# One block of the scan's input formed by TensorE with B on diagonals, and the scan's PSUM tiles by halves

## The chip, the cores and the metric

The kernel runs on one core of one Trainium2 chip. The metric is the time of one execution on the device in microseconds (us). Everything is in fp32.

## What is computed

Two layers follow each other on 8 images of 64 x 64 x 192. The first (a state-space block with a local convolution and an MLP) is not touched. The second is a two-dimensional selective scan. For each of four directions k it runs over L = 4096 positions, for 384 channels with 16 states each:

```python
def step(hst, inp):
    d, bm, cm, uu = inp
    dA = jnp.exp(d[..., None] * A[None])
    dBu = (d * uu)[..., None] * bm[:, :, None, :]
    hst = dA * hst + dBu
    y = jnp.einsum('bkdn,bkn->bkd', hst, cm)
    return (hst, y)
```

`d` is the step size of a channel, `uu` its input, `bm` and `cm` are the B and C of the position, one number for each state. The change is about how `dBu` is formed: the product of `d * uu` (a channel and a position) with B (a state and a position).

## The kernel before

The second layer goes through the images one after the other. A front (projection, 3 x 3 convolution, stores to DRAM in three layouts) comes first, mixed with the finish of the image before. Then `main()` in `scan` runs alone: it is an order written out by hand, kept on every engine.

The scan of an image has 32 **steps**: four directions k, eight chunks of 512 positions (`TT`). A step has 24 **units**: 8 pairs of states p, times 3 groups d of 128 channels. A unit works on two tiles of 128 partitions (the halves f = 0, 1): 2 states x 64 channels on the partitions, 512 positions along the row. Units of a step are numbered 0 to 23 in this document, and iteration u is what the loop in `main` issues for unit u. In iteration u these instructions go out:

- SP: `load_c` (every third unit) loads C of the next pair, broadcast over 64 partitions, into `cb` (three buffers).
- DVE: `run(u)` makes two scans, `hs` from the decay `ea` and the input `g`, each over 512 positions (L1633).
- POOL: `run(u)` copies the last column to `cy` (L1645) and multiplies `hs` with `cb` to `hc` (L1647).
- ACT: `decay(u + 2)` makes `ea` by two exponentials of `dr`, the step sizes repeated over the partitions (L1606). Then come 3, 3 or 2 calls of `weigh` (L1591). One call takes a block j of 128 positions of `duT` (d * uu with positions on the partitions, 384 channels along the row) and scales it with one column of `bt`, which is B of one state with positions on the partitions. It writes one half of `pw`. A pair of states needs 4 blocks x 2 states = 8 calls, and the `todo` list runs ahead of their use by 10 calls.
- PE: `supply(u + 1)` turns the eight blocks of `pw` (2 halves x 4 blocks, 128 x 128 each) by transposes into the PSUM tile `g` of the next unit (L1617). `collect(u - 1)` then sums `hc` over the two states by a product with `sel`, into `y` (L1662); both halves of `y` are 64 columns wide. In direction 0 the first pair adds the skip term first (L1660).
- The pieces of `prepare(s + 1)`, which make the next step's inputs, are hung on fixed units: `project` (PE, `p_d`) on 2, 3 and 4, `keep` (DVE copy to `xdbl`, store of C to DRAM) on 5, `turn_b` on 6, `keep_b` and `step(0)` (PE, `p_dt`) on 7, and so on to 17; copies to `dr` on 11, 20 and 21.

The PSUM tiles of `g` are `[128, 2, 512]`, two banks, and there are two of them. All PSUM is used: four banks for `g`, three for `y`, one for the pieces.

All DMAs of the scan are issued from SP, in the order of the program; an issue that waits holds up what is behind it.

Of the kernel before, what the change touches and what calls it, by code (L numbers as in the profile page):

```python
# [8 lines left out]
F32 = mybir.dt.float32  # L9
AF = mybir.ActivationFunctionType  # L10
ALU = mybir.AluOpType
PSUM = bass.MemoryType.PSUM
DRAM = bass.MemoryType.DRAM
# [4 lines left out]
TT = 512  # L18
# [6 lines left out]
DT = DIN // 128  # L25

K, N, R = 4, 16, 12
NS1 = NT
NB1 = TT // 128
NP1 = N // 2  # L30

EXPLN = "natural_log_exp_and_others"

# [60 lines left out]
class Flow:  # L94
# [24 lines left out]
    def pool(self, tag, n):  # L119
        self.slots[tag] = [0.0] * n  # L120
# [911 lines left out]
def layer1(tc, consts, x1s, mv1, out, w_in, w_x, w_dt, w_out):  # L1032
    nc = tc.nc
# [6 lines left out]
    with ExitStack() as ctx:  # L1040
# [3 lines left out]
        mp = pool("m1", 1, space=PSUM)  # L1044
        dp = pool("d1", 3, space=DRAM)
        ddp = pool("dd1", 2, space=DRAM)
        yacc = pool("ya1", 1, side="right").tile([128, DT, L], F32, name="yacc")

        wi = wp.tile([CP, CT, 2 * DIN], F32, name="wi1")
# [28 lines left out]
        for m in range(2 * DT):  # L1078
            for ct in range(CT):
# [4 lines left out]
                    start=ct == 0,  # L1084
# [3 lines left out]
        nc.vector.tensor_copy(gb.rearrange("p m b -> p (m b)"), pb[:, : 2 * DT * nb])  # L1088
        keeper = []
        o = lambda ins: keeper[-1](ins)  # L1090

        def scaled(w, b, half):

# [340 lines left out]
        def scan(xo):  # L1434
# [7 lines left out]
            def spool(name, bufs, **kw):  # L1442
                pools[name] = cx.enter_context(tc.tile_pool(name=name, bufs=bufs, reuse_waits="tile", **kw))

            steps = [(k, c) for k in range(K) for c in (range(NS1) if k < 2 else range(NS1 - 1, -1, -1))]
            units = [(s, p, d) for s in range(len(steps)) for p in range(NP1) for d in range(DT)]
            state = [dict() for _ in steps]
            made = {}

# [3 lines left out]
            def prepare(s, bank=lambda name: mp.tile([128, TT], F32, name=name, tag="mm")):  # L1453
# [31 lines left out]
                def keep():  # L1485
                    xd = xds[s % 2]
                    o(nc.vector.tensor_copy(xd[0:44], st["p_d"][:44]))
                    st["cd"] = dp.tile([N, TT], F32, name="cd")
                    o(nc.sync.dma_start(out=st["cd"], in_=xd[16:32]))

                def turn_b():
                    xd = xds[s % 2]
# [43 lines left out]
                def keep_du(d):  # L1536
# [10 lines left out]
                    2: [(project, 0)],  # L1547
                    3: [(project, 1)],
                    4: [(project, 2)],
                    5: [(keep,)],  # L1550
                    6: [(turn_b,)],
                    7: [(keep_b,), (step, 0)],
                    8: [(soft, 0)],
# [56 lines left out]

            def supply(u):
                s, p, d = units[u]
                made["g", u] = g = pools["g1"].tile([128, 2, TT], F32, name="g")
                for f in range(2):
                    for j in range(NB1):
                        o(
                            nc.tensor.transpose(  # L1617
                                g[:, f, j * 128 : j * 128 + 128],
                                state[s]["pw", p, j][:, 2 * d + f].rearrange("p a b -> p (a b)"),
                                ident,  # L1620
                            )
                        )

            def run(u):
                s, p, d = units[u]
                k, c = steps[s]
                st = state[s]
                ea, g = made.pop(("e", u)), made.pop(("g", u))
                h = pools["h1"].tile([128, 2, TT], F32, name="hs")
                rev = (lambda ap: ap) if k < 2 else (lambda ap: ap[:, ::-1])  # L1630
                for f in range(2):
                    o(
                        nc.vector.tensor_tensor_scan(  # L1633
                            rev(h[:, f]),
                            rev(ea[:, f]),
                            rev(g[:, f]),
                            0.0 if first(s) else state[s - 1]["cy"][:, p, d, f : f + 1],
                            ALU.mult,
                            ALU.add,
                        )  # L1640
                    )
                if "cy" not in st:
                    st["cy"] = pools["pr1"].tile([128, NP1, DT, 2], F32, name="cy")
                last = TT - 1 if k < 2 else 0
                o(nc.gpsimd.tensor_copy(st["cy"][:, p, d], h[:, :, last]))  # L1645
                made["hc", u] = hc = pools["h1"].tile([128, 2, TT], F32, name="hc")
                o(nc.gpsimd.tensor_mul(hc, h, bc(st["cb", p], 1, [128, 2, TT])))  # L1647

            def collect(u):
                s, p, d = units[u]  # L1650
                k, c = steps[s]
                st = state[s]
                if p == 0:
                    st["y", d] = pools["y1"].tile([128, TT], F32, name=f"y{d}")
                y = st["y", d]
                hc = made.pop(("hc", u))
                half = [slice(f * 64, f * 64 + 64) for f in range(2)]
                if p == 0 and k == 0:
                    for f in range(2):
                        o(nc.tensor.matmul(y[half[f]], dskip[:, d, half[f]], st["xc"][:, d], start=True, stop=False))  # L1660
                for f in range(2):
                    o(nc.tensor.matmul(y[half[f]], sel, hc[:, f], start=p == 0 and k > 0, stop=p == NP1 - 1))  # L1662

            def add(u):
                s, p, d = units[u]
                k, c = steps[s]
                if p == NP1 - 1:
                    ya = view(yacc, k, d, c * TT, TT)
                    yv = seq(state[s]["y", d], k)
                    if k == 0:  # L1670
                        o(nc.vector.tensor_copy(ya, yv))
                    else:
                        o(nc.vector.tensor_add(ya, ya, yv))


            todo = [
                (s, p, j, i) for s in range(len(steps)) for p in range(NP1) for j in range(NB1) for i in range(2)
            ]

            def prologue(f, mq, front_pools):  # L1680

                yield "wait", "front"
                front_pools.close()
                for name, n in (("pr1", 2), ("dr1", 4), ("pw1", 8), ("bc1", 3), ("e1", 3)):
                    spool(name, n)
                load_first = prepare(0, lambda name: mq.tile([128, TT], F32, name=name, tag="mm"))
                ready.update({fn.__name__: fn for at in sorted(load_first) for fn, *_ in load_first[at]})
                r = yield step("SP", 0.1, ready["load"])
                yield "take", "mm"
                r += 3.5  # L1690
                for d in range(DT):
                    r = yield step("PE", 0.95, lambda: ready["project"](d), r)
                r = yield step("DVE", 0.7, ready["keep"])
                f.give("mm", r)
                f.at["xd"] = r
                yield "take", "mm"
                yield step("PE", 0.6, ready["turn_b"])
                r = yield step("DVE", 0.2, ready["keep_b"])
                f.give("mm", r)
                f.at["bt"] = r  # L1700
                load_c(0, 0)
                for d in range(DT):
                    yield "wait", ("du", d)
                for t in todo[:10]:
                    yield step("ACT", 0.55, lambda: weigh(*t), f.free["ACT"])
                for u in range(2):
                    yield step("ACT", 1.35, lambda: decay(u), None, "explog")
# [17 lines left out]
                f.at["du", d] = r  # L1725

            def main():
                for name, n, kw in (("h1", 3, {}), ("y1", 1, dict(space=PSUM)), ("g1", 2, dict(space=PSUM))):
                    spool(name, n, **kw)
                supply(0)  # L1730
                rest = iter(todo[10:])
                nu = len(units)
                for u, (s, p, d) in enumerate(units):
                    if p == 0 and d == 0:
                        pieces = prepare(s + 1) if s + 1 < len(steps) else {}
                    s2, p2 = (s, p + 1) if p < NP1 - 1 else (s + 1, 0)
                    if s2 < len(steps) and d == 0:
                        load_c(s2, p2)
                    run(u)
                    if u + 2 < nu:  # L1740
                        decay(u + 2)
                    for _ in range((3, 3, 2)[d]):
                        if t := next(rest, None):
                            weigh(*t)
                    if u + 1 < nu:
                        supply(u + 1)
                    if u >= 1:
                        collect(u - 1)
                    if u >= 2:
                        add(u - 2)  # L1750
                    for f, *args in pieces.get(p * DT + d, ()):
                        f(*args)
                collect(nu - 1)
                add(nu - 2)
                add(nu - 1)
                cx.close()
# [136 lines left out]
```

## Time and profile before

| | us |
|---|---|
| median of 3 runs | 23702.0 |
| lowest, highest run | 23690.56, 23706.31 |
| the profiled execution's own time | 23706.31 |
| its span | 23706.3 |

The first layer takes up to about 4,780 us of the span. Each image's scan takes about 2,100 us (the first from 5009 to 7112 us), with a front of about 250 us between two of them. One step of the scan takes 66.5 us in direction 0 and 65.55 us in the three others.

How to read it: the page gives busy time, which is an average over all stages. For a change in the scan the rows of a stretch inside a scan are what counts. A row of the timeline is a start, a duration, an engine, a line, an operation and its tiles (out<-in), and in brackets the time that the engine had been idle before and what ended it. PE records carry a tail after the array has finished, so their ends overlap; starts of the weight loads (PEld) tell better when PE was free.

### The profile page before, as it was taken

How to read it: one execution, taken by the hardware profiler on the slowest of the kernel's cores; microseconds unless marked ns; L12 is line 12 of the kernel's file. 1: busy time of each engine (PE TensorE's matmuls, PEld its weight loads, DVE VectorE, ACT ScalarE, POOL GpSimd, SP SyncE). 2: the span in 40 equal slices, each digit the busy share in tenths (PEclk: the TensorE clock that was granted, in tenths of full speed). 3: DMA queues.
4: the chain of work that ended last, by engine and by line, in shares of the span. 5: the costliest groups of instructions: out<-in, count | busy, mean ns of one | idle time of the engine just before them, and what ended most of it. 6: DMA issues, size and time to landing. Idle time of an engine off the chain costs nothing.

```text
span 23706.3 us, 312102 instructions
## 1 busy us (share of the span) xinstructions
PE 21012.6 (89%) x100356; PEld 10233.4 (43%) x100356; DVE 21257.2 (90%) x22093; ACT 20961.7 (88%) x37466; POOL 16001.1 (67%) x12871
## 2 busy tenths in 40 slices
PE   8999999978888888888888888888888888888888
PEld 4444444434444444444444444444444444444444
DVE  7888888779998999899989998999899989998998
ACT  5666666679998999899989998999899989998998
POOL 1111111159995998599859986997699769976997
PEclk8999999989999999999999999999999999999999
DMA  1111111133233322332233233322333333333332
GB/s 51 44 44 44 45 45 46 36 101 81 82 78 112 81 81 77 110 82 81 77 108 81 81 80 111 81 81 78 108 81 82 84 102 81 82 86 100 82 82 67
DMA packets 1205983, 1859.70 MB, mean 78 GB/s; under 512 B 268960, under 2 KB 502336, under 8 KB 1195136
## 3 DMA queue, kind: packets, MB, share of 16 engines
q1 hardware_dynamic: 1204352, 1839.73, 28.5%
q8 instruction: 807, 13.22, 0.2%
q14 instruction: 824, 6.75, 0.1%
HBM read 1225.98 MB, written 210.50 MB: 61 GB/s over the span
## 4 chain that ended last, share of the span: by engine, by line
POOL 46%; PE 22%; ACT 13%; DVE 8%; issue 6%; DMA 3%; SPq 1%; POOLq 0%; ACTq 0%; DVEq 0%
POOL hc L1647 43%; ACT pw L1591 5%; ACT ea L1606 5%; POOL cy L1645 3%; PE p_f L955 3%; DVE xs L1201 2%; DMA xc<-xo 2%; PE p_x L448 2%; PE p_f L975 2%; PE y L1662 2%; PE p_o L872 1%; PE g L1617 1%; PE p_y L789 1%; PE p_d L1480 1%; PE p_z L531 1%
## 5 line engine op out<-in xcount | busy, mean ns | idle before, releaser
L1647 POOL TENSOR_TENSOR hc<-hs,cb 128x1024 f32<-128x1024 f32 x6144 | 14577.6, 2373 | 12.3 <-POOL cy L1645 10.5
L1633 DVE TENSOR_TENSOR_SCAN hs<-ea,cy,g 128x512 f32<-128x512 f32 x10752 | 13027.1, 1262 | 602.4 <-PE g L1617 408.7
L1591 ACT ACTIVATE pw<-duT,bt 128x384 f32<-128x384 f32 x16384 | 8875.4, 601 | 23.5 <-DVE duT L1538 23.5
L1606 ACT ACTIVATE ea<-dr,an 128x512 f32<-128x512 f32 x12288 | 8121.7, 709 | 186.9 <-DVE hs L1633 169.5
L1662 PE MATMUL y<-hc,sel 128*64 128x512 f32 x24576 | 6628.6, 618 | 1836.3 <-POOL hc L1647 1816.1
L1617 PEld LDWEIGHTS g<-ident,pw 128*128 128x128 f32 x49152 | 5288.2, 141 | 4335.1 <-issue 2666.3
L1617 PE MATMUL g<-ident,pw 128*128 128x128 f32 x49152 | 6788.1, 279 | 60.8 <-ACT pw L1591 29.3
L1645 POOL COPY cy<-hs 128x2 f32<-128x2 f32 x6144 | 1150.7, 187 | 3394.4 <-DMA out_x<-xl 1744.8
L1662 PEld LDWEIGHTS y<-hc,sel 128*64 128x64 f32 x24576 | 1226.6, 135 | 3250.6 <-POOL hc L1647 3025.0
L1633 DVE TENSOR_TENSOR_SCAN hs<-ea,g 128x512 f32<-128x512 f32 x1536 | 1764.2, 1203 | 160.9 <-PE g L1617 119.6
L365 POOL TENSOR_TENSOR s<-xs 96x512 f32<-96x512 f32 x64 | 121.7, 1902 | 2136.0 <-DVE xs L343 1846.6
L1201 DVE SCALAR_TENSOR_TENSOR xs<-pad,p,xs 128x4096 f32<-128x4096 f32 x192 | 860.9, 4484 | 48.0 <-ACT xs L1191 40.8
L1509 PE MATMUL p_dt<-xdbl,wd 13*128 13x512 f32 x1536 | 857.5, 639 | 41.8 <-DVE de L1522 39.9
L365 POOL TENSOR_TENSOR s<-sq 96x512 f32<-96x512 f32 x128 | 180.4, 1409 | 937.9 <-ACT sq L378 842.3
L1480 PE MATMUL p_d<-xc,wx 128*44 128x512 f32 x1536 | 788.7, 596 | 23.4 <-DMA xc<-xo 23.4
L343 DVE SCALAR_TENSOR_TENSOR x<-xx,p,x 96x512 f32<-96x512 f32 x1024 | 784.4, 815 | 15.2 <-ACT x L332 15.0
L955 PE MATMUL p_f<-h,wf 96*128 96x512 f32 x1536 | 757.2, 631 | 43.8 <-ACT zs L550 27.4
L343 DVE SCALAR_TENSOR_TENSOR xs<-xin,p,xs 96x512 f32<-96x512 f32 x1024 | 746.9, 768 | 3.6 <-ACT xs L332 3.6
L975 PE MATMUL p_f<-m,wf 128*96 128x512 f32 x1536 | 695.0, 603 | 0.0
L1531 PEld LDWEIGHTS p_du<-ident,de 128*128 128x128 f32 x3072 | 323.4, 141 | 610.1 <-DVE de L1522 406.3
L365 POOL TENSOR_TENSOR s<-x 96x512 f32<-96x512 f32 x64 | 109.1, 1704 | 690.3 <-DVE x L343 606.7
L448 PE MATMUL p_x<-h,wi 96*128 96x512 f32 x1024 | 559.4, 679 | 12.0 <-ACT h L405 12.0
(202 smaller groups left out, 19293.3 us busy)
## 6 DMA issues: line engine op xcount, KB each, us to landing
cb<-cd SPq DMA_DIRECT2D x4096, 128.0 KB
dr<-de SPq DMA_DIRECT2D x3072, 128.0 KB
xc<-xo SPq DMA_DIRECT2D x256, 768.0 KB
e<-csd SPq DMA_DIRECT2D x256, 384.0 KB
xl<-x SPq DMA_DIRECT2D x256, 384.0 KB
ut<-xo SPq DMA_DIRECT2D x128, 768.0 KB
ut<-xo SPq DMA_DIRECT2D x256, 384.0 KB
xo<-xs SPq DMA_DIRECT2D x48, 1024.0 KB
```

The lines of the kernel that those rows point to most:

```text
L343: nc.vector.scalar_tensor_tensor(im(out[:, ct]), tap(ct, j), w[:, ct, j : j + 1], im(out[:, ct]), ALU.mult, ALU.add)
L448: nc.tensor.matmul(ps, wi[:, ct, 390 + mt * 128 : 518 + mt * 128], h[:, ct], start=ct == 0, stop=ct == 1)
L955: nc.tensor.matmul(ps, wf1[:, ct, mt * 128 : mt * 128 + 128], h[:, ct], start=ct == 0, stop=ct == 1)
L975: nc.tensor.matmul(ps[:CP], wf2[:, kt, ct * CP : ct * CP + CP], m[:, kt], start=kt == 0, stop=kt == 5)
L1201: nc.vector.scalar_tensor_tensor(xs, tap(j), kw[:, d, j : j + 1], xs, ALU.mult, ALU.add)
L1591: nc.scalar.activation(st["pw", p, j][:, :, i], st["duT"][:, j].rearrange("p (g c) -> p g c", c=64), AF.Copy, scale=st["bt"][:, j, n : n + 1],
L1606: nc.scalar.activation(ea[:, f], state[s]["dr", d][:, f], AF.Exp, scale=an[:, k, p, at : at + 1])
L1617: nc.tensor.transpose(g[:, f, j * 128 : j * 128 + 128], state[s]["pw", p, j][:, 2 * d + f].rearrange("p a b -> p (a b)"), ident,)
L1633: nc.vector.tensor_tensor_scan(rev(h[:, f]), rev(ea[:, f]), rev(g[:, f]), 0.0 if first(s) else state[s - 1]["cy"][:, p, d, f : f + 1], ALU ...
L1645: o(nc.gpsimd.tensor_copy(st["cy"][:, p, d], h[:, :, last]))
L1647: o(nc.gpsimd.tensor_mul(hc, h, bc(st["cb", p], 1, [128, 2, TT])))
L1662: o(nc.tensor.matmul(y[half[f]], sel, hc[:, f], start=p == 0 and k > 0, stop=p == NP1 - 1))
```

## The change

Pairs 4 to 7 (states 8 to 15) are treated in a new way for block j = 0; the other blocks of these pairs, and all blocks of pairs 0 to 3, stay as they were.

- **Diagonals.** For each step, `spread` (a new piece on unit 5) writes B of 8 states at the first 128 positions onto the diagonals of 8 matrices of 128 x 128 in DRAM (`dz`, two of them, zeroed once at the start of the layer), by one DMA of 1,024 single elements. A second DMA loads all 8 matrices into `dg` (512 KB). The first step of an image has its `spread` at the start of `main`.
- **Product.** In `supply`, a unit of these pairs forms block 0 of each half by two matmuls with 64 channels of `duT` as weights and a diagonal matrix as the moving operand; each writes 64 partitions. They stand before the three transposes of that half.
- **Weighing.** The 8 calls of `weigh` a step for these blocks (4 pairs x 2 states) fall away.
- **Order.** The pairs run as 0, 4, 1, 5, 2, 6, 3, 7, so units of the two kinds come three by three. A pair of the new kind issues 2 calls of `weigh` in each of its units, one of the old kind 3, 3 and 2 as before.
- **Halves.** `g` is a tile of one bank for each half, with four buffers.

Counted in the two programs: ACT has 2,048 instructions fewer, PE 6,144 more matmuls (12,288 new products for 6,144 transposes), SP 514 DMAs more, POOL one instruction more (the zeroing), DVE as many as before.

```diff
+ND = 8
+ORDER = [0, 4, 1, 5, 2, 6, 3, 7]
...
+        zero = yacc[:, 0, : ND * 128].rearrange("p (n b) -> p n b", b=128)
+        nc.gpsimd.memset(zero, 0.0)
+        dzs = [dgp.tile([ND, 128 * 128], F32, name=f"dz{i}") for i in range(2)]
+        for t in dzs:
+            nc.sync.dma_start(out=t.rearrange("n (a b) -> a n b", b=128), in_=zero)
...
-            units = [(s, p, d) for s in range(len(steps)) for p in range(NP1) for d in range(DT)]
+            units = [(s, p, d) for s in range(len(steps)) for p in ORDER for d in range(DT)]
...
+                def spread():
+                    dz = dzs[s % 2]
+                    st["dg"] = dg = pools["dg1"].tile([128, ND, 128], F32, name="dg")
+                    o(nc.sync.dma_start(out=dz[:, :: 128 + 1], in_=xds[s % 2][N - ND : N, 0:128]))
+                    o(nc.sync.dma_start(out=dg, in_=dz.rearrange("n (a b) -> a n b", b=128)))
...
-                    5: [(keep,)],
+                    5: [(keep,), (spread,)],
...
             def supply(u):
                 s, p, d = units[u]
-                made["g", u] = g = pools["g1"].tile([128, 2, TT], F32, name="g")
                 for f in range(2):
+                    made["g", u, f] = g = pools["g1"].tile([128, TT], F32, name="g")
                     for j in range(NB1):
+                        if on_diagonal(p, j):
+                            for i in range(2):
+                                o(
+                                    nc.tensor.matmul(
+                                        g[i * 64 : i * 64 + 64, j * 128 : j * 128 + 128],
+                                        state[s]["duT"][:, j, (2 * d + f) * 64 : (2 * d + f) * 64 + 64],
+                                        state[s]["dg"][:, 2 * p + i - (N - ND)],
+                                        start=True,
+                                        stop=True,
+                                    )
+                                )
+                            continue
                         o(
                             nc.tensor.transpose(
-                                g[:, f, j * 128 : j * 128 + 128],
+                                g[:, j * 128 : j * 128 + 128],
                                 state[s]["pw", p, j][:, 2 * d + f].rearrange("p a b -> p (a b)"),
                                 ident,
                             )
...
+            def on_diagonal(p, j):
+                return j == 0 and 2 * p >= N - ND
+
             todo = [
-                (s, p, j, i) for s in range(len(steps)) for p in range(NP1) for j in range(NB1) for i in range(2)
+                (s, p, j, i)
+                for s in range(len(steps))
+                for p in ORDER
+                for j in range(NB1)
+                for i in range(2)
+                if not on_diagonal(p, j)
             ]
...
-                for name, n, kw in (("h1", 3, {}), ("y1", 1, dict(space=PSUM)), ("g1", 2, dict(space=PSUM))):
+                for name, n, kw in (("dg1", 2, {}), ("h1", 3, {}), ("y1", 1, dict(space=PSUM)), ("g1", 4, dict(space=PSUM))):
                     spool(name, n, **kw)
+                ready["spread"]()
                 supply(0)
...
-                    for _ in range((3, 3, 2)[d]):
+                    for _ in range(((2, 2, 2) if on_diagonal(p, 0) else (3, 3, 2))[d]):
                         if t := next(rest, None):
                             weigh(*t)
```

More of the change, by code (lines that the diff above doesn't have):

```diff
@@ L1046, in layer1 @@
         ddp = pool("dd1", 2, space=DRAM)
+        dgp = pool("dg1", 1, space=DRAM)
         yacc = pool("ya1", 1, side="right").tile([128, DT, L], F32, name="yacc")
@@ L1627, in run @@
                 st = state[s]
-                ea, g = made.pop(("e", u)), made.pop(("g", u))
+                ea, g = made.pop(("e", u)), [made.pop(("g", u, f)) for f in range(2)]
                 h = pools["h1"].tile([128, 2, TT], F32, name="hs")
@@ L1635, in run @@
                             rev(ea[:, f]),
-                            rev(g[:, f]),
+                            rev(g[f]),
                             0.0 if first(s) else state[s - 1]["cy"][:, p, d, f : f + 1],
@@ L1652, in collect @@
                 st = state[s]
-                if p == 0:
+                if p == ORDER[0]:
                     st["y", d] = pools["y1"].tile([128, TT], F32, name=f"y{d}")
@@ L1657, in collect @@
                 half = [slice(f * 64, f * 64 + 64) for f in range(2)]
-                if p == 0 and k == 0:
+                if p == ORDER[0] and k == 0:
                     for f in range(2):
@@ L1661, in collect @@
                 for f in range(2):
-                    o(nc.tensor.matmul(y[half[f]], sel, hc[:, f], start=p == 0 and k > 0, stop=p == NP1 - 1))
+                    o(nc.tensor.matmul(y[half[f]], sel, hc[:, f], start=p == ORDER[0] and k > 0, stop=p == ORDER[-1]))
             def add(u):
@@ L1666, in add @@
                 k, c = steps[s]
-                if p == NP1 - 1:
+                if p == ORDER[-1]:
                     ya = view(yacc, k, d, c * TT, TT)
@@ L1700, in prologue @@
                 f.at["bt"] = r
-                load_c(0, 0)
+                load_c(0, ORDER[0])
                 for d in range(DT):
@@ L1733, in main @@
                 for u, (s, p, d) in enumerate(units):
-                    if p == 0 and d == 0:
+                    q = u % (NP1 * DT)
+                    if q == 0:
                         pieces = prepare(s + 1) if s + 1 < len(steps) else {}
-                    s2, p2 = (s, p + 1) if p < NP1 - 1 else (s + 1, 0)
+                    s2, p2, _ = units[u + DT - d] if u + DT - d < nu else (len(steps), 0, 0)
                     if s2 < len(steps) and d == 0:
@@ L1750, in main @@
                         add(u - 2)
-                    for f, *args in pieces.get(p * DT + d, ()):
+                    for f, *args in pieces.get(q, ()):
                         f(*args)
```

## The prediction

> **What bounds the kernel now.** I read the busy times first, then busy time by stretch, then the timeline of one step of the scan. The page:
>
> ```profile
> PE 21012.6 (89%) x100356; PEld 10233.4 (43%) x100356; DVE 21257.2 (90%) x22093; ACT 20961.7 (88%) x37466; POOL 16001.1 (67%) x12871
> ...
> L1633 DVE TENSOR_TENSOR_SCAN hs<-ea,cy,g 128x512 f32<-128x512 f32 x10752 | 13027.1, 1262 | 602.4 <-PE g L1617 408.7
> L1591 ACT ACTIVATE pw<-duT,bt 128x384 f32<-128x384 f32 x16384 | 8875.4, 601 | 23.5 <-DVE duT L1538 23.5
> ...
> L1662 PE MATMUL y<-hc,sel 128*64 128x512 f32 x24576 | 6628.6, 618 | 1836.3 <-POOL hc L1647 1816.1
> ...
> L1617 PE MATMUL g<-ident,pw 128*128 128x128 f32 x49152 | 6788.1, 279 | 60.8 <-ACT pw L1591 29.3
> ```
>
> Three engines are near 90%, so the average decides nothing. By stretch (columns: us, then busy us and instructions of PE, PEld, DVE, ACT, POOL); the first lies in direction k=0, the second in k=1:
>
> ```profile
> 7600.00:7800.00 200.00, 181.10 (x990) 88.16 (x988) 190.03 (x178) 196.57 (x356) 180.15 (x145) 1.00 0.29 80
> ...
> 8200.00:8400.00 200.00, 175.88 (x965) 86.86 (x964) 192.94 (x180) 199.47 (x361) 182.74 (x147) 1.00 0.32 82
> ```
>
> ACT is full and DVE 96%: it looks ACT-bound. The timeline of one step (k=1, 24 units, 8023.76 to 8089.31, so 65.55 us) corrects this:
>
> ```profile
> 8036.58 0.86 PEld L1617 LDWEIGHTS g<-ident,pw 128*128 128x128 f32 x8 [0.83 <-PE y L1662]
> ...
> 8037.61 0.20 PEld L1662 LDWEIGHTS y<-hc,sel 128*64 128x64 f32 x4 [0.17 <-POOL cy L1645]
> ...
> 8037.81 2.45 DVE L1633 TENSOR_TENSOR_SCAN hs<-ea,cy,g 128x512 f32<-128x512 f32 x2 [0.49 <-PE g L1617]
> ...
> 8040.87 0.31 SPq L1489 DMA_DIRECT2D cd<-xdbl  x1
> 8041.27 2.67 SPq L1579 DMA_DIRECT2D cb<-cd  x4
> ...
> 8043.44 2.37 POOL L1647 TENSOR_TENSOR hc<-hs,cb 128x1024 f32<-128x1024 f32 x1
> ...
> 8045.86 1.08 PE L1662 MATMUL y<-hc,sel 128*64 128x512 f32 x4 [0.53 <-POOL hc L1647]
> ...
> 8046.87 1.12 PE L1509 MATMUL p_dt<-xdbl,wd 13*128 13x512 f32 x2
> ...
> 8047.92 1.09 PE L1617 MATMUL g<-ident,pw 128*128 128x128 f32 x8
> ...
> 8048.94 0.20 PEld L1662 LDWEIGHTS y<-hc,sel 128*64 128x64 f32 x4 [0.17 <-issue]
> 8049.15 2.45 DVE L1633 TENSOR_TENSOR_SCAN hs<-ea,cy,g 128x512 f32<-128x512 f32 x2 [1.14 <-PE g L1617]
> ```
>
> The last row is unit 9. Its chain is PE's: hc(6), y(6), the piece p_dt, the eight transposes, then the scan 0.14 us after the last. DVE's own work is 24 x 2.36 (scan pairs) + 10 pieces x 0.59 + 0.16 = 62.6 us; the other 3.0 us are waits: 0.51 and 0.58 at units 4 and 5 (PE, behind p_d), 1.2 at unit 9 (PE), 0.16 at unit 14, and 0.47 at units 21 to 23, where g waits for ACT's pw. So ACT sets only the last; most of the loss is PE's chain.
>
> **What the Trainium skill says.** "TensorEngine Tiling (Array Packing)", Restrictions: column tiling rules out transpose mode for fp32. So the new product runs as a true fp32 multiply; the trace shows those as two passes (four y records for two matmuls). "TensorE: Matmul & The Clock Gate", Part 3, The mechanism: tiles in different columns run together, and a weight load passes a running matmul only where the row group differs. The trace agrees in effect: y's four passes end in 1.08 us where one pass of 512 takes 0.43 (two p_d loads, 8032.26 and 8032.69), and between y (64 columns) and g (128) the load waits: 1.01 us from y to g is two passes, 0.86, plus 0.15; 1.03 from g to y is 8 x 0.107 + 0.17. "DMA: Bandwidth & Descriptors", Rules for kernel authors: a strided last dimension makes one descriptor per element, and a DMA that reads what another wrote must wait for its completion. No run here shows such a scatter.
>
> **The change part by part.**
>
> *ACT.* 8 of 64 weighings a step go (2,048 in all): 1.51 us for three to the next ea gives 0.50 each, 4.0 us a step. Off the path except at units 21 to 23: gain 0.47.
>
> *PSUM by halves.* The first scan of a unit waits for four transposes, not eight: 4 x 0.107 = 0.43 earlier. The second half follows before the first scan's 1.19 us are over. Four one-bank tiles hold what two two-bank tiles did; each half now waits for its own scan of two units before, which is long done.
>
> *PE.* In 12 of 24 units each half has two 64-column products (four passes of 128 columns, 0.107 each, two at a time: 0.21) for one transpose (0.107): +0.21 a unit. The second half's block lies between transposes: two more changes of tile shape, 0.15 to 0.17, +0.31. Sum **+0.52** a unit, 6.2 us a step. The first half's block follows y or p_d in y's own shape, without a change (k=0's dskip and y passes run 0.43 apart). Bounds: +0.21 if a change costs nothing; +0.95 if the halves don't run together. I take 0.52, since both sides were measured on y.
>
> With L the first load of g: before, scan at L+1.23 and next y at L+1.03. After, plain unit: scan L+0.79, y L+1.03. Diagonal: scan L+0.90, y L+1.55; behind p_dt or p_du, whose shape differs, scan L+1.05, y L+1.70. The step above (8000 dropped; old starts in brackets):
> - y(1) 31.78, p_d, L4 = 33.64: scan 4 at 34.54 (34.87).
> - y(2) 33.64 + 1.55 = 35.19, + 1.01 + 0.85 for p_d, L5 = 37.05: scan 5 at 37.95 (37.81).
> - y(3) 38.60, third p_d to 40.6, DVE's keep 0.59: scan 6 at 41.2 (40.77). DVE then runs: scan 7 43.58, scan 8 46.11.
> - hc(6) ends 43.58 + 0.29 + 2.37 = 46.24, y(6) 46.29, p_dt, L9 = 48.35: scan 9 at 49.40 (49.15).
> - y(7) 50.05, L10 = 51.06; scan 10 behind delta at 52.35 (52.10).
> - y(8) 52.61, p_dt, L11 = 54.67: scan 11 at 55.72 (54.52). **Here 1.2 us is lost:** PE has been behind since unit 3.
> - Units 12 to 20 are DVE's own; the 0.16 at unit 14 and the 0.47 at units 21 to 23 come back. Net +0.6 a step.
>
> At k=0 dskip's passes (0.86 a unit) stand before y(1) and y(2) on a PE now without slack: 1.72, where before it cost 66.5 - 65.55 = 0.95. Net +0.6 + 1.72 - 0.95 = +1.4.
>
> *Transfers.* SP gets 512 more: per step a scatter of 1,024 four-byte elements and a load of 512 KB. The load waits on SP for the scatter to land; cb for unit 9 is queued behind it, and POOL's hc(9) waits for that. DMA packets of 4 to 256 B take 9 to 25 ns here; 8 rows let 8 engines share, 128 elements each, 1.2 to 3.2 us, plus 1.35 us that a store to csd takes until the next load issues: 2.5 to 4.6 us. Then cb issues at about 47, lands by 51.5 (load 1.8 us of 512-byte packets at 27 ns), and hc(9) wants it at 52.1. Hidden, barely. Cost 0; at 60 ns an element (my outer bound, no row shows it) cb is 4.7 late and unit 12 some 2.4.
>
> *Starts.* At each image's first step xc (issued 7362.50) stands behind scatter and load, and p_d already waited for it at 7370.38: about 4 us x 8 = 32. Zeroing the two DRAM tiles: about 5 once.
>
> *Order of pairs.* It spreads diagonal units and weighings; same count, cost 0 (ACT covers).
>
> **Sum.** 192 steps x 0.6 = 115, 64 x 1.4 = 90, 32, 5: +242. The profiled execution took 23706.31 us, its span 23706.3; it is one of the three runs (median 23702.0, 4 less), so 23702 + 242 = **23,940**.
>
> **Rivals.**
> - *PE's chain loosens (faster), 0.23.* If changes of shape cost nothing there, the gain of halves wins: unit 9 0.5 earlier, unit 11 likewise, units 14 and 21 to 23 free: -1.2 x 192, about -0.5 x 64, +37 = 23,480. At most ACT's 4.0 us are worth DVE's 3.0 of waiting: 22,940. For it: ACT 99.7% busy. Against: unit 9's row names PE. It decides where a diagonal unit costs PE under about 0.3 us.
> - *The blocks run one after another, 0.09.* +0.95 a unit: unit 11 loses 1.9 more, units 21 to 23 0.9: +2.8 x 256 on the main case = 24,660. Against: y's halves run together.
> - *The scatter is slow, 0.12.* POOL waits for cb: 2.4 x 256 on the main case = 24,560. From about 5 us on.
> - *It does not do what it says*: SP would run on, and the order shows the wait, so no share apart.
>
> **How the numbers follow.** Main case 0.50 (its own range 23,750 to 24,200), the other three above, and 0.06 for gains and losses that cancel. A measurement can tell about 0.2%, 47 us, from no change. Faster 0.23, same 0.06, slower 0.71. The range 23,440 to 24,640 takes in most of the faster case and the scatter.
>
> **What would show it.** Right: ACT's share in the scan falls to some 93%, PE rises over 94%; waits of the scan for g at units 5, 9 and 11; in the second half of a diagonal unit 0.15 us before and after the block; k=0 steps near 68, others 66.1 us. Wrong: steps under 65 us; blocks back to back with transposes; hc waiting for cb.

## The result and the profile after

The changed kernel takes 23952.97 us (median of 4 runs, 23949.37 to 23973.23); the kernel before, in the same runs, 23704.15 us (median of 4). The ratio is 1.0108, with a 95% interval of 1.0094 to 1.0121: about 1.1% slower. The forecast was 23,940 us.

The page of the kernel after, busy times and then the costliest groups (busy us, mean ns, idle time before and what ended it):

```profile
PE 22479.0 (94%) x118788; PEld 10970.5 (46%) x118788; DVE 21258.0 (89%) x22093; ACT 20266.4 (85%) x35418; POOL 15994.0 (67%) x12872
...
L1659 DVE TENSOR_TENSOR_SCAN hs<-ea,cy,g 128x512 f32<-128x512 f32 x10752 | 12994.3, 1263 | 772.2 <-PE g L1643 698.3
...
L1605 ACT ACTIVATE pw<-duT,bt 128x384 f32<-128x384 f32 x14336 | 7832.5, 600 | 25.1 <-DVE duT L1552 25.1
L1688 PE MATMUL y<-hc,sel 128*64 128x512 f32 x24576 | 6624.4, 617 | 695.9 <-POOL hc L1673 651.6
L1643 PE MATMUL g<-ident,pw 128*128 128x128 f32 x43008 | 6693.9, 284 | 7.9 <-DVE hs L1659 4.3
...
L1633 PE MATMUL g<-dg,duT 128*64 128x128 f32 x24576 | 2796.5, 290 | 25.8 <-DMA dg<-dz 25.0
```

ScalarE did get lighter: 2,048 weighings and 695 us of busy time are gone. It bought next to nothing, as a run below shows. VectorE's work is the same to 1 us, but its scans now wait 772 us where they waited 602, and 698 of that is for `g` from TensorE, after 409. TensorE's own idle time ahead of `y` fell from 1,836 to 696 us: most of the slack that it had is used up. The stretches inside a scan (us, then busy us and instructions of PE, PEld, DVE, ACT, POOL; k = 0, then k = 1):

```profile
7600.00:7800.00 200.00, 194.25 (x1178) 94.59 (x1177) 185.82 (x175) 184.41 (x325) 176.43 (x143) 1.00 0.32 86
8200.00:8400.00 200.00, 191.24 (x1168) 94.02 (x1164) 190.14 (x179) 188.67 (x332) 180.31 (x146) 1.00 0.35 90
```

In the second row TensorE went from 175.9 to 191.2 us of 200, ScalarE from 199.5 to 188.7, VectorE from 192.9 to 190.1: now TensorE is the busiest engine, and the step is longer.

Summed over the two profiled executions, with a step counted from its first scan to the next step's first, the difference of the spans splits like this:

| part | before | after | difference | forecast |
|---|---|---|---|---|
| 192 steps with k of 1 to 3 | 12543.1 | 12686.1 | +143.0 | +115 |
| 64 steps with k = 0 | 4262.7 | 4385.5 | +122.8 | +90 and +32 for the starts |
| all ahead of, between and after the scans | 6900.5 | 6883.1 | -17.4 | +5 |
| span | 23706.3 | 23954.7 | +248.4 | +242 |

The times from scan to scan of a step with k = 1 or more (median us from the first scan of unit n-1 to that of unit n, from the records of the scans) show where it goes. The diagonal units (those of pairs 4 to 7) are 3 to 5, 9 to 11, 15 to 17 and 21 to 23. The units that are left out of the table differ by at most 0.03 us:

| unit n | 4 | 5 | 6 | 9 | 11 | 14 | 21 | 22 | 23 | whole step |
|---|---|---|---|---|---|---|---|---|---|---|
| before | 2.87 | 2.94 | 2.95 | 3.57 | 2.42 | 2.52 | 2.64 | 2.45 | 2.46 | 65.55 |
| after | 2.54 | 3.40 | 3.26 | 3.37 | 3.39 | 2.36 | 2.34 | 2.53 | 2.55 | 66.45 |

The timeline of the kernel after, from `y` of unit 6 to the scan of unit 9 and `y` of unit 7 (start, duration, engine, line, in brackets the idle time before). A "block" is what the products form in place of one transpose; each has four loads, two matmuls of two passes:

```profile
8087.12 0.20 PEld L1688 LDWEIGHTS y<-hc,sel 128*64 128x64 f32 x4 [0.61 <-POOL hc L1673]
...
8088.13 0.29 PEld L1523 LDWEIGHTS p_dt<-xdbl,wd 13*128 13x128 f32 x2 [0.81 <-DVE hs L1659]
...
8089.18 0.20 PEld L1633 LDWEIGHTS g<-dg,duT 128*64 128x64 f32 x4 [0.76 <-issue]
...
8089.55 0.31 PEld L1643 LDWEIGHTS g<-ident,pw 128*128 128x128 f32 x3 [0.17 <-issue]
...
8090.03 0.20 PEld L1633 LDWEIGHTS g<-dg,duT 128*64 128x64 f32 x4 [0.17 <-issue]
...
8090.21 2.45 DVE L1659 TENSOR_TENSOR_SCAN hs<-ea,cy,g 128x512 f32<-128x512 f32 x2 [0.92 <-PE g L1643]
...
8090.40 0.31 PEld L1643 LDWEIGHTS g<-ident,pw 128*128 128x128 f32 x3 [0.17 <-issue]
...
8090.87 0.20 PEld L1688 LDWEIGHTS y<-hc,sel 128*64 128x64 f32 x4 [0.17 <-issue]
```

The four loads of a block start 0.37 us ahead of the transposes behind them (8089.18 to 8089.55): 0.20 us with loads and 0.17 without one. Three transposes take 0.31 and are again followed by 0.17. From the first block to the next `y` it is 8090.87 - 8089.18 = 1.69 us. The forecast had 1.70. The Trainium skill, "TensorEngine Tiling (Array Packing)", Key Properties, says that a change of the tiling mode drains TensorE. The trace fits this: 0.17 us without a load at each change between blocks of 64 columns and transposes of 128. What happens in the array meanwhile, no row shows.

### The profile page after: what moved, and what is told of

It is laid out like the page before. It is cut to its first block, busy times and chain, and to the rows that moved or that the text cites. A ratio compares the mean times of both kernels' runs of the same rounds, so it can differ in the third digit from the quotient of the medians.

```text
span 23954.7 us, 348547 instructions
## 1 busy us (share of the span) xinstructions
PE 22479.0 (94%) x118788; PEld 10970.5 (46%) x118788; DVE 21258.0 (89%) x22093; ACT 20266.4 (85%) x35418; POOL 15994.0 (67%) x12872
## 5 line engine op out<-in xcount | busy, mean ns | idle before, releaser
L1605 ACT ACTIVATE pw<-duT,bt 128x384 f32<-128x384 f32 x14336 | 7832.5, 600 | 25.1 <-DVE duT L1552 25.1
L1643 PE MATMUL g<-ident,pw 128*128 128x128 f32 x43008 | 6693.9, 284 | 7.9 <-DVE hs L1659 4.3
L1643 PEld LDWEIGHTS g<-ident,pw 128*128 128x128 f32 x43008 | 4562.3, 141 | 2940.3 <-issue 1420.1
L1633 PE MATMUL g<-dg,duT 128*64 128x128 f32 x24576 | 2796.5, 290 | 25.8 <-DMA dg<-dz 25.0
L1633 PEld LDWEIGHTS g<-dg,duT 128*64 128x64 f32 x24576 | 1514.0, 136 | 2270.4 <-issue 2170.5
```

Source lines behind the costliest of these rows:

```text
L1605: nc.scalar.activation(st["pw", p, j][:, :, i], st["duT"][:, j].rearrange("p (g c) -> p g c", c=64), AF.Copy, scale=st["bt"][:, j, n : n + 1],
L1633: nc.tensor.matmul(g[i * 64 : i * 64 + 64, j * 128 : j * 128 + 128], state[s]["duT"][:, j, (2 * d + f) * 64 : (2 * d + f) * 64 + 64], stat ...
L1643: nc.tensor.transpose(g[:, j * 128 : j * 128 + 128], state[s]["pw", p, j][:, 2 * d + f].rearrange("p a b -> p (a b)"), ident,)
```

## The experiments

A kernel is named by what it does; "a step" is the median step with k of 1 or more, unless k = 0 is said. A "diagonal unit" is one of the pairs that are on diagonals in that kernel. Each ratio is to the kernel before, measured beside the experiment: 23706.34 us for the first four, 23710.9 for the next four and 23698.33 for the last two.

### The halves alone

The kernel before, with only the split of `g`:

```diff
-                made["g", u] = g = pools["g1"].tile([128, 2, TT], F32, name="g")
                 for f in range(2):
+                    made["g", u, f] = g = pools["g1"].tile([128, TT], F32, name="g")
...
-("g1", 2, dict(space=PSUM))
+("g1", 4, dict(space=PSUM))
```

> The kernel before with one part of the change: g as four one-bank tiles, one for each half. My theory (the scan waits on the chain through TensorE, and the halves shorten it by 0.43 us, but ACT's own work of 65.2 us a step stops the gain): the waits at units 4, 5 and 9 shrink by 0.4 us each and a step of k=1 to 3 falls from 65.55 to about 65.2 us, k=0 from 66.5 to about 65.7; 0.4 to 0.6% faster, 23,570 to 23,620 us. Rival A (only the chain counts, ACT has room): -1.1 us a step, 1.2% faster, about 23,420. Rival B (ACT alone set the pace): no change, 23,700.

Measured: 23615.35 us, ratio 0.9960 (0.9945 to 0.9974), a step 65.24 us, k = 0 66.07 (expected about 65.7). Unit 9 now takes 3.11 us after 3.57, and unit 4 2.43 after 2.87. But units 12 and 15 now take 3.53 and 3.56, where they took 2.95 before. Its timeline before unit 15 shows who is late:

```profile
8183.08 0.31 PEld L1617 LDWEIGHTS g<-ident,pw 128*128 128x128 f32 x3 [0.81 <-ACT pw L1591]
...
8184.06 0.53 PEld L1617 LDWEIGHTS g<-ident,pw 128*128 128x128 f32 x5 [0.67 <-ACT pw L1591]
...
8185.18 0.69 DVE L1522 SCALAR_TENSOR_TENSOR de<-spa,p_dt 128x512 f32<-128x512 f32 x1 [0.53 <-ACT spa L1517]
```

TensorE's transposes stop in the middle of a unit for ScalarE's `pw`, and VectorE's `delta` waits for ScalarE's `spa`. With TensorE's chain shortened, ScalarE is the next bound, 0.3 us a step further down. So the halves are a gain by themselves. Units 21 to 23 take 2.38, 2.37 and 2.37 here, with all of ScalarE's weighings still made. No run took weighings away without the halves.

### Everything but the products

The kernel after, in which block 0 of a diagonal unit is formed by a transpose of `pw` of block 1:

```diff
-                        if on_diagonal(p, j):
-                            for i in range(2):
-                                o(nc.tensor.matmul(...))
-                            continue
...
-                                state[s]["pw", p, j][:, 2 * d + f]...
+                                state[s]["pw", p, 1 if on_diagonal(p, j) else j][:, 2 * d + f]...
```

> The changed kernel without the products: block 0 of the units on diagonals is a transpose of pw's block 1 again (so these blocks hold wrong values; B of states 8 to 15 at the first 128 positions is left out). ACT's relief, the halves, the order and the transfers stay. My theory (the products are the loss, 0.52 us of TensorE a unit): k=1 to 3 falls from 66.45 to about 64 us, k=0 from 67.9 to about 65; about 23,330, 1.6% faster than before. Rival A (transfers on SP and their traffic are the loss): it stays near 66 us a step, 23,850 to 23,950. Rival B (the loss lies in the order of pairs): the same, no gain over the changed kernel.

Measured: 23320.0 us, ratio 0.9836 (0.9819 to 0.9852), a step 63.96, k = 0 65.13. The page of this kernel has the scan waiting 328 us in all:

```profile
L1647 DVE TENSOR_TENSOR_SCAN hs<-ea,cy,g 128x512 f32<-128x512 f32 x10752 | 12945.4, 1261 | 328.1 <-PE g L1631 230.2
```

So halves, the relief of ScalarE, the order of pairs and the transfers together would bring 1.6 us a step. The products, against transposes in their place, take all of it and 0.9 more: 66.45 - 63.96 = 2.5 us a step for 12 units, out of 12 x 0.52 = 6.2 us of TensorE's time.

### The transfers only once an image

The kernel after, with scatter and load only in an image's first step:

```diff
                 def spread():
+                    if s:
+                        st["dg"] = state[s - 1]["dg"]
+                        return
                     dz = dzs[s % 2]
```

> The changed kernel with scatter and load in the first step of each image alone; later steps use the first step's diagonals (wrong values of B in these blocks from the second step on). My theory (the scatter's 3.5 us of waiting on SP and the 512 KB are hidden): steps stay at 66.4 and 67.9 us, first steps near 73; 23,940 to 23,955, the same as the changed kernel within 0.1%. Rival (cb comes late behind the scatter, or the load crowds the queues): steps fall by 0.3 us or more, below 23,880.

Measured: 23961.22 us, ratio 1.0106 (1.0091 to 1.0121), a step 66.45, k = 0 67.9: the kernel after, in every step. The transfers cost nothing inside a scan. In the kernel after, the queue of SP waits for the scatter like this (waits in the engine's own queue: us in total, times, longest; then SP's issues at unit 6):

```profile
SPq L1503 <- DMA dz<-xdbl: 830.4, 256, 3.9
```

```profile
8082.42 0.32 SPq L1502 DMA_DIRECT2D dz<-xdbl  x1
...
8086.24 0.39 SPq L1503 DMA_DIRECT2D dg<-dz  x1
...
8086.73 2.44 SPq L1593 DMA_DIRECT2D cb<-cd  x4
```

The mean wait is 830.4 / 256 = 3.2 us. `hc` of unit 9 did not wait for `cb`: it needed it at about 8092.9 us, 6 us after the issue.

### Both halves' blocks together

The kernel after, with the blocks of both halves ahead of all six transposes: two changes of tile shape fewer in a diagonal unit:

```diff
                 for f in range(2):
                     made["g", u, f] = g = pools["g1"].tile([128, TT], F32, name="g")
                     for j in range(NB1):
                         if on_diagonal(p, j):
                             for i in range(2):
...
+                for f in range(2):
+                    g = made["g", u, f]
+                    for j in range(NB1):
+                        if on_diagonal(p, j):
                             continue
                         o(
                             nc.tensor.transpose(
```

> The changed kernel with the blocks of both halves ahead of the six transposes: one change of tile shape a unit less on the way in and one less on the way out, same work. My theory (a change of shape costs 0.15 us on TensorE): a diagonal unit costs 0.31 us less (2.25 instead of 2.56 us from y to y), the first half is ready 0.22 us later; k=1 to 3 about 65.4 us, k=0 about 67.1; 23,740 to 23,790, within 0.4% of before. Rival (the cost is the fp32 passes themselves, and order on TensorE does not matter): y to y stays at 2.56 us, 23,950 or, by the later first half, more.

Measured: 23737.83 us, ratio 1.0013 (1.0004 to 1.0021), a step 65.70, k = 0 66.83. The page of this kernel, and its timeline where unit 22 is supplied:

```profile
L1663 DVE TENSOR_TENSOR_SCAN hs<-ea,cy,g 128x512 f32<-128x512 f32 x10752 | 13007.6, 1261 | 640.8 <-PE g L1647 556.2
```

```profile
8744.40 0.14 PEld L1633 LDWEIGHTS g<-dg,duT 128*64 128x64 f32 x2 [0.29 <-issue]
...
8744.83 0.36 PEld L1633 LDWEIGHTS g<-dg,duT 128*64 128x64 f32 x6 [0.29 <-issue]
...
8745.36 0.64 PEld L1647 LDWEIGHTS g<-ident,pw 128*128 128x128 f32 x6 [0.17 <-issue]
```

The eight loads of both halves' blocks follow each other, and there is one change between them and the six transposes, where the kernel after has three. (The gap after the first two loads is no change: those two start while `y` still runs.) At unit 5, where TensorE goes from `y` to `y` without a wait, the unit takes 3.10 us after 3.40: 0.30 for two changes, with the same products and transposes. So the rival (the passes themselves, whatever their order) falls. Units 4 and 9, whose first scan the later first half delays, take 0.22 more (2.76 and 3.59), as expected. Two changes in each of 12 units are 3.7 us of TensorE's time (0.31 for the two, by the forecast); with the later first half set against them, they cost 66.45 - 65.70 = 0.75 us of the step, 215 us of the whole. That is some 0.9 of the 1.1 points that the change lost. The step is still above the kernel before's 65.55, and above the 65.4 that was expected.

### The other order of pairs, with the blocks together and apart

Diagonal units at 0-2, 6-8, 12-14 and 18-20, so that none falls on the products of the projection at units 2 to 4 of the step. First with the blocks together:

```diff
-ORDER = [0, 4, 1, 5, 2, 6, 3, 7]
+ORDER = [4, 0, 5, 1, 6, 2, 7, 3]
```

> The changed kernel with both halves' blocks ahead of the six transposes (as in the run before this one) and the order of pairs 4, 0, 5, 1, 6, 2, 7, 3 in place of 0, 4, 1, 5, 2, 6, 3, 7: the diagonal units are then 0-2, 6-8, 12-14 and 18-20 of a step and not 3-5, 9-11, 15-17 and 21-23, so that none of them meets the products of the projection after units 2 to 4. Theory (a diagonal unit costs the end only where TensorE has no slack beside it): the waits at units 5 and 11 go, a step with k of 1 or more takes 64.3 us (64.0 to 64.9) after 65.7, one with k = 0 66.0; the first unit of an image now needs the diagonals at once, so that each image starts 5 to 9 us later: 23,475 us in all (23,430 to 23,570). Rival (only TensorE's sum counts, not where the units lie): 65.7 a step as in the run before, 23,740 and more.

Measured: 23657.94 us, ratio 0.9978 (0.9969 to 0.9987), a step 65.06, k = 0 66.47. The waits at units 5 and 11 are gone (2.94 and 2.36), as the theory had it, but unit 14 has a new one of 0.8 (3.17), units 6 and 8 new ones of 0.2, and a front between two images takes 261 us, not 249. So place counts, by 0.64 us a step; the size was wrong by 0.8, most of it at unit 14, where I had overlooked the piece that stands after unit 12.

The same order on the kernel after:

> The changed kernel with the order of pairs 4, 0, 5, 1, 6, 2, 7, 3 alone; each half's blocks stay ahead of its own three transposes, with four changes of tile shape in a diagonal unit. Theory of place: TensorE's waits move from units 4, 5 and 11 to wherever a diagonal unit meets other pieces (units 6-8, with the turn of B), but become smaller: 65.8 us a step (65.2 to 66.2) after 66.45, 67.4 with k = 0, image starts 5 to 9 us later, 23,840 us in all (23,740 to 23,930). Rival (the sum of TensorE's work decides): 66.45 a step as in the changed kernel, 23,990 with the later starts.

Measured: 23953.35 us, ratio 1.0102 (1.0085 to 1.0119): no different from the kernel after. A step is 66.05, k = 0 67.94. The waits moved as expected (units 5, 6 and 11 back to 2.94, 2.96 and 2.36; units 8, 9 and 14 at 3.05, 3.47 and 3.25), but they became only 0.4 us smaller, and the fronts, 261 us after 248, took it back. The expected 23,840 us were not reached. Two orders were tried; whether a third has a better place for a diagonal unit with four changes of shape is open.

### ScalarE's relief taken back

The kernel after, in which ScalarE still makes the 8 weighings a step, unread:

```diff
-                if not on_diagonal(p, j)
...
-                    for _ in range(((2, 2, 2) if on_diagonal(p, 0) else (3, 3, 2))[d]):
+                    for _ in range((3, 3, 2)[d]):
```

> The changed kernel in which ScalarE still weighs the blocks that the diagonals replace (3, 3 and 2 weighings a unit everywhere, 64 a step in place of 56); their results are not read. It takes ScalarE's relief away and leaves the rest. Theory (TensorE's chain sets the changed step and ScalarE's relief is worth only what its last units waited for): 66.45 us a step becomes 66.9 (66.5 to 67.3), 24,070 us in all (23,970 to 24,170). Rival (ScalarE is the bound, and its relief carries the change): a step grows by the whole 2.6 us of weighing, to 69, 24,600 us.

Measured: 23971.28 us, ratio 1.0110 (1.0095 to 1.0125), a step 66.45 us, k = 0 67.92. Both theories fell, mine too: every unit of the step takes what it took in the kernel after, within 0.01 us. The page:

```profile
PE 22500.0 (94%) x118788; PEld 10975.0 (46%) x118788; DVE 21256.4 (89%) x22093; ACT 20992.2 (88%) x37466; POOL 16005.4 (67%) x12872
...
L1659 DVE TENSOR_TENSOR_SCAN hs<-ea,cy,g 128x512 f32<-128x512 f32 x10752 | 12989.8, 1262 | 780.6 <-PE g L1643 683.6
```

ScalarE has 726 us more to do than in the kernel after, and the scan waits as long as there. In the changed kernel the relief of ScalarE is worth nothing in a step that prepares the next. The last step of an image, which prepares none, does show it: 60.67 us with the weighings, 59.76 without, 7 us in all.

### Two pairs, at two places

Blocks together, and only pairs 6 and 7 on diagonals, at units 12-14 and 18-20:

```diff
-ND = 8
-ORDER = [0, 4, 1, 5, 2, 6, 3, 7]
+ND = 4
+ORDER = [0, 1, 2, 3, 6, 4, 7, 5]
```

> Blocks together, and only two pairs of states (6 and 7, ND = 4) on diagonals, laid at the fifth and the seventh place of a step (order 0, 1, 2, 3, 6, 4, 7, 5), units 12-14 and 18-20, where VectorE's own pieces make the units longer and TensorE waits. Half the relief of ScalarE, half the products. Theory (the kernel with the halves alone is held at 65.24 a step by ScalarE, at units 12 and 15; 1.3 us less of weighing clears these waits, and TensorE has room for six diagonal units there): 64.2 us (63.9 to 64.7) a step, 65.2 with k = 0, no later start of an image; 23,360 us in all (23,320 to 23,480), faster than every kernel here that does the whole computation. Rival (every diagonal unit costs its 0.3 to 0.5 us wherever it lies): 65.2 less the waits of ScalarE of 1.1 plus 6 x 0.3 gives 65.9, 23,780.

Measured: 23528.82 us, ratio 0.9923 (0.9909 to 0.9938), a step 64.80, k = 0 65.97. Every unit takes what it takes without products, except unit 14: 3.17 for 2.36. That puts the run above the expected 23,320 to 23,480. Its timeline:

```profile
8670.00 0.29 PEld L1523 LDWEIGHTS p_dt<-xdbl,wd 13*128 13x128 f32 x2 [0.81 <-DVE duT L1552]
...
8671.05 0.42 PEld L1633 LDWEIGHTS g<-dg,duT 128*64 128x64 f32 x8 [0.76 <-issue]
...
8671.64 0.64 PEld L1647 LDWEIGHTS g<-ident,pw 128*128 128x128 f32 x6 [0.17 <-issue]
...
8672.32 2.45 DVE L1663 TENSOR_TENSOR_SCAN hs<-ea,cy,g 128x512 f32<-128x512 f32 x2 [0.74 <-PE g L1647]
```

The third product of `step`, issued after unit 12, stands between `y` and the blocks of unit 14. The three diagonal units 18 to 20, where TensorE has no piece, cost nothing. First steps still took 70.1 us (median; 69.5 to 71.8, and 66.7 in the first image), with no product before unit 12. The reason is in the timeline of an image's start: the next step's `xc` is issued behind the wait for the scatter, and the projection waits for it:

```profile
7326.75 0.35 SPq L1502 DMA_DIRECT2D dz<-xdbl  x1
7330.86 0.38 SPq L1503 DMA_DIRECT2D dg<-dz  x1
...
7332.48 0.60 SPq L1469 DMA_DIRECT2D xc<-xo  x1
```

```profile
7339.72 1.28 PE L1488 MATMUL p_d<-xc,wx 128*44 128x512 f32 x2 [4.48 <-DMA xc<-xo]
```

The next run answers to both: the pairs at units 15-20, and the image's first `spread` issued behind unit 0's pieces.

```diff
-ORDER = [0, 1, 2, 3, 6, 4, 7, 5]
+ORDER = [0, 1, 2, 3, 4, 6, 7, 5]
...
-                ready["spread"]()
                 supply(0)
...
                     for f, *args in pieces.get(q, ()):
                         f(*args)
+                    if u == 0:
+                        ready["spread"]()
```

> As the run with two pairs on diagonals, but these pairs at the sixth and seventh place of a step (order 0, 1, 2, 3, 4, 6, 7, 5; units 15-20, where TensorE has one piece, the turn after unit 16, in place of the product of step 2 after unit 12), and the first spread of an image issued behind unit 0's pieces, so that the next step's xc no longer waits on SP's queue for the scatter. Theory (a diagonal unit costs nothing where TensorE has slack; the 0.81 us that the fourteenth scan lost came from the product after unit 12; the 5 us of an image's first step came from SP's order): 64.0 us a step (63.9 to 64.3) after 64.8, 65.2 with k = 0, first steps 65.5 to 66.5 after 70.6; 23,330 us in all (23,290 to 23,420). Rival (ScalarE, relieved of 1.3 us, is full at 63.9 a step, and gets its relief later in the step: its waits at units 12 and 15 come back in part): 64.6 a step, 23,460.

Measured: 23387.1 us (23379.57 to 23402.52), ratio 0.9870 (0.9854 to 0.9887), a step 64.41 (just above the expected 64.3, under the rival's 64.6), k = 0 65.59, first steps 64.3 after 70.1 (not 70.6, as the expectation has it). Only the kernel without the products was faster; this one is 1.3% below the kernel before and 2.4% below the changed one. Unit 14 is back at 2.36, but unit 15 takes 3.38 and not 2.92:

```profile
8645.03 1.61 ACT L1605 ACTIVATE pw<-duT,bt 128x384 f32<-128x384 f32 x3
...
8646.55 0.57 ACT L1530 ACTIVATE spa<-p_dt 128x512 f32<-128x512 f32 x1
...
8647.82 0.69 DVE L1536 SCALAR_TENSOR_TENSOR de<-spa,p_dt 128x512 f32<-128x512 f32 x1 [0.33 <-ACT spa L1531]
```

ScalarE makes three weighings in this unit, where the kernel with the pairs at 12-14 makes two, and only then `spa`, for which `delta` waits. So the rival (ScalarE's waits come back) holds at unit 15 and not at unit 12, and the theory holds for TensorE.

### Three pairs

As the last, with `ND = 6` and the plain order, so that units 15-23 are diagonal.

> As the run beside it, with three pairs on diagonals at the end of the step in the plain order (ND = 6, order 0 to 7; units 15-23). ScalarE is relieved of 2.0 us in place of 1.3, TensorE gets three more diagonal units at 21-23, each of which cost 0.15 us where the blocks were together. Theory: 64.4 us a step (64.1 to 64.7), 65.6 with k = 0, 23,420 us in all (23,360 to 23,480), slower than two pairs. Rival (ScalarE bounds the run with two pairs): faster than two pairs, 64.0 a step, 23,330.

Measured: 23463.5 us, ratio 0.9900 (0.9885 to 0.9915), a step 64.74 (at the upper end of what was expected), k = 0 65.59: slower than two pairs, as the theory had it. Units 21 and 22 take 0.2 and 0.1 us longer than with two pairs. Unit 15 stays at 3.38, with two weighings a step fewer: that wait is one of ScalarE's order, not of its sum.

## Why the prediction was right, and where it was off

The chain through TensorE and its price per unit were right. That the sum came within 13 us of the measured time is in part luck: the steps with k of 1 to 3 cost 28 us more than forecast and the rest around the scans 22 us less.

- **The bound.** The forecast read the waits of the steps as TensorE's chain, although ScalarE was 99.7% busy. The products alone turn 63.96 us a step into 66.45, and taking ScalarE's relief back changes nothing in a step: this holds. ScalarE comes to the front elsewhere: at units 12 and 15 with the halves alone (65.24), and at unit 15 with two or three pairs. (The forecast's sum of VectorE's own work, 62.6 us, comes to 62.7; nothing hangs on it.)
- **The price of a diagonal unit.** +0.52 us: in the timeline 1.69 us from the first block to `y` for 1.70 forecast, and 2.56 from `y` to `y` (8123.59 to 8126.15) for 1.01 + 1.55. The two 64-column products of a block do run together: four loads start within 0.20 us. Two of the changes of shape are worth 0.75 us a step.
- **The chain by units.** The forecast gave the periods to units 4, 5, 6, 9 and 11 as 2.54, 3.41, 3.25, 3.29 and 3.37. Measured were 2.54, 3.40, 3.26, 3.37 and 3.39. Scans of units 5, 9 and 11 wait 0.9 us each for `g`, as forecast; summed up to unit 11 the step is 1.22 us behind that of before, and the forecast saw 1.2 lost there.
- **The end of the step: the term that was mis-sized.** "Units 12 to 20 are DVE's own; the 0.16 at unit 14 and the 0.47 at units 21 to 23 come back." The 0.16 did. Of the 0.47, units 21 to 23 gave 7.56 - 7.42 = 0.14. The forecast put the three diagonal units there at nothing. That needs a TensorE that comes to them with a lead of 0.6 us; the trace shows that it can't build one up:

```profile
8121.04 0.20 PEld L1688 LDWEIGHTS y<-hc,sel 128*64 128x64 f32 x4 [0.98 <-POOL hc L1673]
...
8121.07 2.38 POOL L1673 TENSOR_TENSOR hc<-hs,cb 128x1024 f32<-128x1024 f32 x1
...
8121.53 0.14 PEld L1633 LDWEIGHTS g<-dg,duT 128*64 128x64 f32 x2 [0.29 <-issue]
8121.95 0.39 PE L1633 MATMUL g<-dg,duT 128*64 128x128 f32 x4
...
8123.53 2.38 POOL L1673 TENSOR_TENSOR hc<-hs,cb 128x1024 f32<-128x1024 f32 x1
...
8123.59 0.20 PEld L1688 LDWEIGHTS y<-hc,sel 128*64 128x64 f32 x4 [0.17 <-POOL cy L1671]
...
8126.15 0.20 PEld L1688 LDWEIGHTS y<-hc,sel 128*64 128x64 f32 x4 [0.17 <-POOL cy L1671]
```

`y` waits for `hc`, and the next unit's supply stands behind `y` on TensorE. POOL begins an `hc` every 2.46 us, so TensorE is never further ahead than one unit of POOL. Three diagonal supplies of 2.56 us then meet scans of 2.36 and need 0.6 us; units 22 and 23 take 0.17 and 0.19 more than VectorE's own 2.36, so the lead covered about 0.25. The 0.33 that didn't come back make +0.9 a step out of +0.6. Half of that excess came back in the last step of an image, which prepares no successor and fell from 60.99 to 59.76 us (0.9 of this is ScalarE's relief, by the run with the weighings kept), and in the first step of a direction (65.04 to 65.37): the sum over the 192 steps is +143, for +115.
- **ScalarE's relief.** The weighings' busy time fell by 4.1 us a step (8875.4 to 7832.5 in all), for 4.0 forecast, ScalarE's as a whole only by 2.7; what fills the rest was not looked for. The relief was credited with that 0.47. That was the wrong cause: with the weighings kept, units 21 to 23 take the same 2.34, 2.52 and 2.55, and the halves alone had brought them to 2.38, 2.37 and 2.37. Whether the halves do it, or the waits earlier in the step that let ScalarE catch up, no run tells apart.
- **Weight loads.** The forecast drew on the Trainium skill, "TensorE: Matmul & The Clock Gate", Part 3, The mechanism: a load passes a running matmul only where the row group differs. The same section also lets a load run ahead into a background weight buffer, and the trace shows loads ahead on the same 128 rows: the loads at 8121.53 above start while the passes of `y` run, 0.42 us ahead of their own products at 8121.95. Where the shape changes, no load starts for 0.17 us, so it is the change that goes with the wait. The sum used the measured gaps and does not suffer.
- **k = 0.** +1.4 a step, 67.9 us: 66.5 and 67.9 were measured. Within it the skip term's price is 67.9 - 66.45 = 1.45 and not 1.72, which hides that the rest was 0.9 and not 0.6.
- **Transfers.** Hidden, as forecast; the scatter takes 3.2 us in the mean until the load goes out, inside the 2.5 to 4.6. At most 7 of its packets are under way at once in the step above (from the records of the packets), which fits the forecast's guess of 8 engines. The margin of `cb` was larger than forecast.
- **Starts.** Eight first steps took 45.2 us more, of which 8 x 1.4 belong to k = 0; the remaining 34 answer to the forecast's 32. The mechanism is the forecast's (`xc` behind scatter and load). One thing it did not say: the first diagonal unit has to wait for `dg`, and then runs at half clock. The timeline of the kernel after, and its clock there (PEclk stands after POOL):

```profile
7390.20 0.60 SPq L1469 DMA_DIRECT2D xc<-xo  x1
...
7393.01 0.69 PE L1633 MATMUL g<-dg,duT 128*64 128x128 f32 x4 [3.04 <-DMA dg<-dz]
...
7395.93 1.98 PE L1686 MATMUL y<-xc,dskip 128*64 128x512 f32 x4
```

```profile
7393.00:7399.00 6.00, 5.99 (x22) 2.58 (x23) 2.44 (x2) 2.26 (x5) 2.33 (x3) 0.50 0.92 295
```

This wait stands in place of another and adds little. The kernel without the products has none for `dg`, and its first steps are as much longer, 32 us by the same count. There TensorE waits for `xc`, and then too needs 1.93 us for what takes 1.02 later:

```profile
7320.95 1.93 PE L1488 MATMUL p_d<-xc,wx 128*44 128x512 f32 x2 [4.57 <-DMA xc<-xo]
```

- **What surrounds the scans** became 17 us shorter, for +5 forecast. No experiment looked for a cause, and it need not be an effect: single runs of the kernel before lie up to 33 us apart, and in the experiments, but for the two with the other order of pairs, this part takes 6879 to 6898 us.
- **The rivals.** "TensorE's chain loosens" needed a diagonal unit under about 0.3 us. With the blocks together a diagonal unit costs 0.2 us (unit 5 without the piece's 0.86 is 2.24 from `y` to `y`, a plain unit 2.04), and that kernel still isn't faster than before: for this order of pairs the threshold was too high. The rival comes true with two pairs, laid where TensorE is free. A slow scatter and blocks one after another did not occur.

## What to carry to other kernels

Relieving the engine that looks full pays only if the engine that pays for it has slack at the places where the work lands: count the slack by unit of the schedule, not by the average. Work moved to TensorE should be grouped so that the tile shape changes as seldom as possible, and laid where no other piece stands between two links of the chain. A split of a buffer that lets a consumer start on half of the data can be worth more than the change that it came with, and should be measured by itself.

## What the runs showed of the hardware

- A change between 64-column blocks and 128-column transposes costs TensorE 0.15 us (two changes fewer made unit 5 shorter by 0.30) to 0.17 (the gap in the loads), as much as one and a half transposes of 128 x 128 (0.107).
- After 3.04 us without a matmul TensorE ran at a granted clock of 0.50 for the next 6 us: four passes of `y` took 1.98 us for 1.08. The Trainium skill, "TensorE: Matmul & The Clock Gate", Part 1, says that the clock falls to half after an idle window of about 3.4 us and comes back after at least one window of that length with sustained work. The trace agrees on the fall, after a wait a little shorter; the way back took more than one such window, over 6 us. In that time the work goes at half speed, so a wait of 3 us for a transfer costs TensorE more than itself.
- A scatter of 1,024 single elements of 4 bytes onto diagonals in DRAM released the load behind it after 3.2 us in the mean, and after 3.9 at the longest. What costs is the order on SP's queue: with `xc` behind that wait an image's first step took 70.1 us, with `xc` ahead of it 64.3 (these two kernels also differ in the place of the diagonal units; the gain lies at unit 4, 9.1 us before and 3.8 after).
